# A two-layer graph network with a fast matrix product: one product at full width in the first pair, and new orders of the work

## The chip, the cores and the metric

The kernel runs on one core of one Trainium2 chip. TensorE (PE) multiplies matrices into PSUM, which has eight banks; VectorE (DVE) and ScalarE (ACT) read PSUM and work on SBUF; GpSimd (POOL) works on SBUF alone; SyncE (SP) issues all the DMAs. The metric is the device time of one execution in microseconds, lower being better.

## What is computed

There are 64 graphs, each with 256 nodes of 512 features (`x`), a dense 256x256 matrix `adj` and a mask. Two layers follow each other, all in fp32:

```python
# layer 0
agg = einsum('bij,bjf->bif', adj, x) / maximum(sum(adj, -1), EPS)
x   = layernorm(x + relu(concat([x, agg]) @ W.T))
# layer 1
q, k = split(x @ Wqk, 2);  v = x @ Wv
agg = einsum('bij,bjd->bid', adj, k * mask)
w   = inv_scale * mask * einsum('bid,bid->bi', q, agg)
x   = layernorm(x + softmax(w, axis=1)[:, :, None] * v)
```

The kernel uses that the aggregation commutes with the weights. Before the loop it multiplies the two halves of Wqk into one 512x512 matrix, so that in both layers a graph needs one product of its 512 features with a weight 1024 wide, one aggregation over the nodes, and vector work.

## The kernel before

**Pairs.** The graphs are worked two at a time: 32 pairs, the loop `for j in range(NP)`. In step j, layer 0 of pair j and layer 1 of pair j-1 run interleaved. Step 0 has layer 0 alone; after the loop comes layer 1 of the last pair alone.

**Fast products.** Each layer's weight product is split into 2x2 blocks and done with seven block products P1 to P7 in place of eight (`layer0`, `layer1`, `product`). Five of them, P1 to P5, are split once more in the same way (`inner`): seven matmuls of 256 columns in place of four of 512. P6 and P7 run at full width (`outer`, four matmuls of 512 columns). The price is sums: of the input blocks on POOL (`inner_sums`, `fourth_sums`, `outer_sums`), of the weights once at the start (`weight_sums`: `t1`, `t2`, `t4`, the in-place `b12`, and for each inner product the three arrays i1, i2, i4 and an in-place change of its upper right quarter), and of the results on DVE and ACT, which read one PSUM bank and add into another or into SBUF. The aggregation has seven products as well (`gather`).

**Letters.** The order of the matmuls is written out by hand as strings. Each letter takes the next piece of a product. In layer 0: i is P1, k P5, m P2, p P6, q P7, r P3, s P4, and a to g are the aggregation. In layer 1: J is P1, K P2, H P6, Q P7, N P5, P is product P4, L P3, and A to G the aggregation. S turns the last pair's scores into one row for its softmax, and Z turns the result back. I write K5 for the fifth of the seven pieces of K. The results of pieces 1, 3 and 5 of an inner product are put into the two accumulator banks by DVE or ACT; pieces 4, 6 and 7 (in this order behind 1, 3 and 5) then add their products to the same places by TensorE, so each waits for that add or copy.

**Order of the other engines.** `Plan` records every instruction. `Plan.order` then lists them with a model of costs: TensorE follows the strings nearly (an instruction may pass another by a little), and DVE, ACT, POOL and SP get an order from due times that are worked out backwards from TensorE's. This order is fixed in the program. `waiting` holds work that is recorded once certain letters are used up: `when("QP", ...)` runs after the last Q and the last P.

**Banks.** `HOME` and `HOME9` (last pair) give each letter the bank in which its pieces are made. Only the inner products and the aggregations read these entries. p, q, H and Q are `outer` products, which write straight to the banks of their results.

**Softmax and norms.** `softmax(j-2)` and `norm0(j)` are chains that pass between DVE (sums, `shift`), ACT (`less`, squares into `junk`, `rstd` by a logarithm and an exponential, scaling) and SP. `softmax_last` and the lines after `take(ORDER9, ...)` are the end of the kernel: scores from the last pieces of P, S, a maximum on DVE, exponentials on ACT, Z, then `stt` (add probability times v), a norm, and the stores. `sums_T` makes the combinations of a pair's rows that E and other aggregations read.

Of the kernel before, what the change touches and what calls it, by code (L numbers as in the profile page):

```python
# [16 lines left out]
P = 128  # L17
Q = 32
# [7 lines left out]
INNER = (("P1", "P2", "P5", "P3", "P4"), ("P1", "P2", "P5", "P3", "P4"))  # L26
SLOTS_X = {"P1": 0, "P2": 1, "P5": 2, "P3": 2, "P6": 0, "P7": 1, "P4": 0}
SLOTS_X1 = {"P1": 0, "P2": 1, "P5": 2, "P6": 0, "P7": 1, **({"P3": 2, "P4": 0} if "P7" in INNER[1] else {"P3": 0, "P4": 1})}
W1_BY_GP = ("P5", "P3", "P4")
HOME = "i6 k7 m6 p5 q1 r7 s6 a7 b2 c3 J6 K2 H3 Q5 N7 L7 P6 A6 B4 C5"  # L30
HOME9 = "J6 K6 H3 Q7 N7 L5 P1 A2 B3 C1"
LATE = 4.0
ORDER0 = ("i k i i k k i i i k i k k p m m m m k p m p p m q q r q s q r r s m s s r s s r r r a b s d e g "
          "c f")
ORDER1 = ("i k i k i i k i k i k k i k p m p q p r m q p m m r m s r q m r m q r s s r s r s J J J J s a J "
          "b J s d e c f J H g K K H K K K K N H N N K N H A Q Q D C N E N G P Q Q F P P N P P P B L P L L "
          "L L L L")
ORDER = ("i i k i i i k i i k k p m k m k k p p m r q p r q r q r m m r r s m m q s r s s s J a b s J J J "
         "J J s d e J c H f H K K K K g K Q N K N Q K A H D N C E H G N F Q Q N N B N L L L P P P P L P P "
         "L P L L")  # L40
ORDER9 = ("A J C D E J J G J J J J K B H H K K H N N H Q Q K N Q N F N N K K K Q P P P P P P P N L S L Z L "
          "L L L L")


class Step:
# [274 lines left out]
def resnorm_kernel(  # L320
# [13 lines left out]
    B, N, F = x.shape  # L334
    A = wqk_t.shape[0] // 2
    NT, NF, NA = N // P, F // P, A // P
    H, HF = NF // 2, F // 2
# [63 lines left out]
    def v_of(j):  # L401
        return shared[:, 2 * N_SIDE:].rearrange("p (k t f) -> p k t f", k=2, t=NT)
# [56 lines left out]
    for bank in (*banks[0], *(b for pair in banks for b in pair)):  # L459
        mm(bank.rearrange("p (a n) -> p a n", n=P), ones,  # L460
           ones[:, None, :].to_broadcast([P, F // P, P]), start=True)

    def weight_sums(w, name, layer, by_gp=()):
        b11, b21, b12, b22 = (w[:, k * H:(k + 1) * H, :] for k in range(4))
        t1, t2, t4 = (mem.tile([P, H, F], F32, name=f"{name}{k}") for k in (1, 2, 4))
        it = [mem.tile([P, len(INNER[layer]), HF], F32, name=f"{name}i{r}") for r in (1, 2, 4)]
        sides = {"P4": t4, "P6": t2, "P7": b12}
        sub = vec.tensor_sub

        def inner_of(p, b):  # L470
            if p not in INNER[layer]:
                return
            n = INNER[layer].index(p)
            sub = gp.tensor_sub if p in by_gp else vec.tensor_sub
            c11, c12, c21, c22 = (b[:, e, h * HF:(h + 1) * HF] for e in range(2) for h in range(2))
            i1, i2, i4 = (i[:, n] for i in it)
            sides[p] = {"B11": c11, "B21": c21, "B22": c22, "T3": c12, "T1": i1, "T2": i2, "T4": i4}
            sub(i1, c12, c11)
            sub(i2, c22, i1)
            sub(c12, c22, c12)  # L480
            sub(i4, c21, i2)
        sub(t1, b12, b11)
        inner_of("P1", b11)
        sub(t2, b22, t1)
        inner_of("P5", t1)
        sub(b12, b22, b12)
        sub(t4, b21, t2)
        inner_of("P2", b21)
        inner_of("P6", t2)
        inner_of("P7", b12)  # L490
        inner_of("P3", b22)
        inner_of("P4", t4)
        return sides
# [111 lines left out]
        return [first, common, second, second_row, third, fourth_sum, last]  # L605

    def product(layer, p, X, sides, w, q, done, onto=None):
        if p in INNER[layer]:
            return inner(p, X, sides, w, q, lambda: [done(k) for k in range(2)], onto)
        return outer(q, 0, X, BLOCK[p], sides[p], done) + outer(q, 1, X, BLOCK[p], sides[p], done)  # L610

    def outer(ps, k, X, slot, b, done=None):
        def unit(e):
            def go():
                mm(ps[k], X.chunk(slot, k, e), b[:, e])
                if e == H - 1 and done:
                    done(k)
            return go
        return [unit(e) for e in range(H)]
# [294 lines left out]
    W1 = weight_sums(w1, "t1_", 1, W1_BY_GP)  # L914
# [5 lines left out]
    for j in range(NP):  # L920
        X = Xs.pop(j)
        own = owns[j] = ring("own", [P, 2, NT, F], 3)
        u, y, o = pf, py, pu
        ys[j] = ring("y", [P, 2, NT, F])
        at = homes(HOME)
        units, made = layer0(j, X, o, u, y, at), Counter()
        sizes = Counter({name: len(parts) for name, parts in units.items()})
        waiting = []

        def when(done, work):  # L930
            waiting.append((full(done, sizes), work))

        def start_gather0():
            units.update(gather("abcdefg", sumsA.pop(j), sums_T(ys[j]), at["a"], at["c"], at["b"],
                                own=own, rdeg=rdegs.pop(j)))

        def end_gather0():
            place = norm0(j)
            mask_adj(j)
            if place:  # L940
                when("P.L" if j else "", place)

        def x_sums(*ps):
            for p in ps:
                if p in INNER[0]:
                    inner_sums(X, p)

        def next_x():
            if j == 0:
                pass  # L950
            elif j < NP - 1:
                load_xT(j + 1)
            if j < NP - 1:
                inner_sums(Xs[j + 1], None)
                outer_sums(Xs[j + 1], gp)
                inner_sums(Xs[j + 1], "P5")

        def next_adj():
            if j < NP - 1:
                load_adj(j + 1)  # L960
                sumsA[j + 1] = adj_sums(j + 1, 0)
        if j > 0:
            load_x(j)
        if 0 < j < NP - 1:
            load_rows(j + 1)
            degrees(j + 1)
        when("k", lambda: (fourth_sums(X), x_sums("P3")))
        when("i", lambda: x_sums("P6"))
        when("m", lambda: x_sums("P7"))
        when("p" if "P6" in INNER[0] else "i", lambda: x_sums("P4"))  # L970
        when("pqr", start_gather0)
        when("rs", next_x)
        when("abcdefg", end_gather0)
        if j == 0:
            when("abcdefg", next_adj)
        else:
            Y = x1Ts.pop(j - 1)
            u2, o2, y2 = o, pf, y
            vs[j - 1], aggs[j - 1] = v_of(j - 1), agg_of(j - 1)
            q_at = ys[j][:, :, 0]  # L980
            new, dots = layer1(j - 1, Y, q_at, o2, u2, y2, at)
            sizes.update({name: len(parts) for name, parts in new.items()})
            made["L"] = sizes["L"] - len(ahead)
            ahead += new.pop("L")
            units.update(new, L=ahead)

            def y_sums(*ps):
                for p in ps:
                    if p in INNER[1]:
                        inner_sums(Y, p)  # L990

            def start_layer1():
                if j == 1:
                    for k in range(2):
                        turn_here(Y, owns[0], k, o)
                    mask_adj(0)
                else:
                    softmax(j - 2)
                sumsM[j - 1] = adj_sums(j - 1, 1)
                inner_sums(Y, None)  # L1000
                outer_sums(Y, vec)
                inner_sums(Y, "P5")

            def start_gather1():
                units.update(gather("ABCDEFG", sumsM.pop(j - 1), T[0], at["A"], at["C"], at["B"],
                                    aggs[j - 1]))
            when("L" if j > 1 else "m", start_layer1)
            when("J", lambda: y_sums("P6"))
            when("K", lambda: y_sums("P7" if "P7" in INNER[1] else "P4"))
            when("H", lambda: (fourth_sums(Y), y_sums("P4" if "P7" in INNER[1] else "P3")))  # L1010
            if "P7" in INNER[1]:
                when("HN", lambda: y_sums("P3"))
            T = []
            when("ikmpqrs" if j == 1 else "", lambda: T.append(sums_T(owns[j - 1], aggs[j - 1])))
            when("gK", start_gather1)
            when("BFK", dots)
            when("ABCDEFG", next_adj)
        take((ORDER0, ORDER1)[j] if j < 2 else ORDER, units, made, waiting)
        if j > 0:
            py, pu = pu, py  # L1020

    j = NP - 1
# [11 lines left out]
    vs[j] = ring("x", [P, 2, NT, F])  # L1034
    at = homes(HOME9)
    units, dots = layer1(j, X, q_at, o, u, y, at)
# [18 lines left out]
    def divide():  # L1055
# [12 lines left out]
        ("BFK", dots))]  # L1068
    take(ORDER9, units, Counter(), waiting)
    p = small("probs", [P, 2, NT], 2)  # L1070
# [51 lines left out]
```

## Time and profile before

| | |
|---|---|
| median of 3 runs | 1848.31 us (1848.0 to 1849.67) |
| the profiled execution | 1848.66 us, with a span of 1846.6 us from first to last instruction |
| granted TensorE clock | 0.997 |
| instructions | 26243, of which 7382 are matmul records |
| ACT busy | 1245.6 us (67%) |
| POOL busy | 994.2 us (54%) |

An fp32 matmul leaves two records. From start to start, a record of 256 columns takes 0.216 us where nothing waits, and one of 512 columns takes 0.429 us; the TensorE timeline shows both throughout. So a matmul of 256 columns costs 0.43 us and one of 512 costs 0.86 us. The duration that the profile gives a record (0.38 us for 256 columns) [...] overlaps the next.

In the steady part, one step takes 56 us. The first 20 us are the product of Wqk's halves, while its data arrive. Step 0 is over at about 47 us and step 1 at about 113 us; the loop ends at about 1803 us, and the last pair takes the rest.

### The profile page before, as it was taken

To read this page: it belongs to the slowest core of one execution; us is meant where nothing else is said; L and a number is where in the kernel's file an instruction comes from. 1 tells how busy PE (TensorE), PEld (TensorE's weight loads), DVE (VectorE), ACT (ScalarE), POOL (GpSimd) and SP (SyncE) were. 2 spreads that over 40 slices of the span, in tenths; PEclk is the share of its full clock that TensorE was granted. 3 is DMA by queue.
4 is the path that set the end of the run, shared out by engine and by line. 5 is a ranking of instruction groups with operands and counts; after the bars stand their busy time and mean duration, and the time that the engine had idled before them with its cause. 6 is when DMAs were issued, how large, how long until landed. Compare 5 with 4: busy or idle time off the path is not lost.

```text
span 1846.6 us, 26243 instructions
## 1 busy us (share of the span) xinstructions
PE 1827.3 (99%) x7382; PEld 1383.0 (75%) x7382; DVE 1526.3 (83%) x3402; ACT 1245.6 (67%) x3243; POOL 994.2 (54%) x1523
## 2 busy tenths in 40 slices
PE   9999999999999999999999999999999999999997
PEld 5767777777777777777777777777777777777775
DVE  7887879788889888888888887887888888988876
ACT  3656776667766668766677766687666776666775
POOL 5755464564554664545655545655546545456432
PEclk9999999999999999999999999999999999999998
DMA  6134324343333343343433343433333433334311
GB/s 238 49 75 116 93 78 110 98 110 101 99 87 98 98 120 93 86 108 88 109 104 101 84 107 90 120 96 92 99 97 99 110 98 87 102 93 115 99 34 52
DMA packets 380720, 181.61 MB, mean 98 GB/s; under 512 B 263712, under 2 KB 345248, under 8 KB 380576
## 3 DMA queue, kind: packets, MB, share of 16 engines
q1 hardware_dynamic: 380576, 179.94, 36.2%
q8 instruction: 59, 0.97, 0.2%
q14 instruction: 85, 0.70, 0.1%
HBM read 114.35 MB, written 34.08 MB: 80 GB/s over the span
## 4 chain that ended last, share of the span: by engine, by line
PE 95%; DVE 3%; ACT 1%; DMA 1%; issue 0%; SPq 0%; DVEq 0%; ACTq 0%
PE bank L369 95%; DVE own L284 1%; DVE bank L284 1%; DMA shared<-wqk_t 1%; ACT junk L284 0%; DVE y L284 0%; ACT own L284 0%; PE bank L375 0%; DVE shared L284 0%; SPq L385 0%; DVE turn L284 0%; ACT shared L284 0%; DVE x L284 0%; ACT fifth L284 0%; ACT y L284 0%
## 5 line engine op out<-in xcount | busy, mean ns | idle before, releaser
L284 DVE TENSOR_TENSOR bank<-bank,fifth 128x256 f32<-128x256 f32 (+1 forms) x576 | 256.3, 455 | 137.2 <-ACT fifth L284 64.9
L284 ACT COPY y<-bank 128x512 f32<-128x512 f32 x256 | 149.4, 585 | 299.1 <-PE bank L369 268.2
L284 POOL TENSOR_TENSOR x1T_i<-x1T 128x128 f32<-128x128 f32 (+1 forms) x128 | 85.5, 677 | 391.7 <-PE bank L369 383.8
L284 ACT COPY bank<-bank 128x256 f32<-128x256 f32 (+1 forms) x352 | 149.7, 426 | 131.0 <-DVE bank L284 76.1
L284 ACT COPY shared<-bank 128x512 f32<-128x512 f32 x314 | 181.5, 583 | 52.3 <-PE bank L369 47.4
L369 PE MATMUL bank<-w,x1T 128*128 128x512 f32 (+1 forms) x512 | 206.5, 486 | 0.0
L284 ACT ACTIVATE own<-own,shift,rstd 128x512 f32<-128x512 f32 x254 | 193.5, 814 | 8.5 <-DVE shift L284 8.5
L369 PE MATMUL bank<-w,xT 128*128 128x256 f32 (+1 forms) x496 | 195.9, 486 | 0.2
L284 ACT ACTIVATE junk<-own,less 128x512 bf16<-128x512 f32 x254 | 183.4, 722 | 3.7
L284 DVE SCALAR_TENSOR_TENSOR own<-bank,rdeg,own 128x256 f32<-128x256 f32 x384 | 173.0, 476 | 9.1 <-PE bank L369 4.2
L369 PE MATMUL bank<-t_i,x1T_i 128*128 128x256 f32 x640 | 180.2, 380 | 0.2
L284 ACT COPY fifth<-bank 128x256 f32<-128x256 f32 x384 | 137.9, 375 | 53.6 <-PE bank L369 52.6
L284 DVE TENSOR_TENSOR y<-bank,y 128x512 f32<-128x512 f32 x192 | 132.3, 689 | 46.4 <-PE bank L369 38.5
L369 PE MATMUL bank<-t_i,xT_i 128*128 128x256 f32 x640 | 168.6, 380 | 0.3 <-DVE y L284 0.3
L284 POOL TENSOR_TENSOR xT_i<-xT 128x128 f32<-128x128 f32 (+1 forms) x126 | 84.6, 671 | 154.0 <-PE bank L369 143.0
L369 PE MATMUL bank<-t,x1T_s 128*128 128x512 f32 (+1 forms) x384 | 164.0, 521 | 0.1
L369 PE MATMUL bank<-t,xT_s 128*128 128x512 f32 (+1 forms) x384 | 159.8, 524 | 0.0
L369 PEld LDWEIGHTS bank<-t_i,xT_i 128*128 128x128 f32 x640 | 120.6, 189 | 46.6 <-POOL xT_i L284 12.2
L369 PEld LDWEIGHTS bank<-t_i,x1T_i 128*128 128x128 f32 x640 | 118.0, 190 | 39.4 <-issue 16.3
L284 DVE TENSOR_TENSOR shared<-bank,shared 128x512 f32<-128x512 f32 (+1 forms) x157 | 136.0, 891 | 10.8 <-PE bank L369 8.5
L284 ACT COPY own<-bank 128x512 f32<-128x512 f32 x192 | 110.2, 594 | 9.3 <-PE bank L369 7.1
L284 POOL TENSOR_TENSOR sa<-adj 128x256 f32<-128x256 f32 x128 | 102.8, 806 | 25.1 <-PE bank L369 15.2
(170 smaller groups left out, 4493.0 us busy)
## 6 DMA issues: line engine op xcount, KB each, us to landing
x<-x SPq DMA_DIRECT2D x64, 512.0 KB, 3.7
xT<-x_t SPq DMA_DIRECT2D x62, 512.0 KB, 3.8
out<-own SPq DMA_DIRECT2D x62, 512.0 KB, 3.0
x1T<-turn SPq DMA_DIRECT2D x480, 64.0 KB, 2.1
turn<-adj SPq DMA_DIRECT2D x64, 256.0 KB, 3.6
adj<-adj_t SPq DMA_DIRECT2D x64, 256.0 KB, 3.5
turn<-dram SPq DMA_DIRECT2D x31, 264.0 KB, 5.1
shared<-wqk_t SPq DMA_DIRECT2D x4, 512.0 KB, 8.4
```

What stands on the lines that cost most here:

```text
L284: self.plan.record(self.name, lambda: call(out, *args, **kwargs), outs, ins, busy, done, port)
L369: plan.record("PE", lambda: nc.tensor.matmul(ps, a, b, start=start, stop=True, skip_group_check=True), [ps], [a, b], busy, busy + 0.165, w ...
```

## The change

Five things are changed.

1. `FULL_FIRST`: at the first use of the layer 1 products, P4 has no inner weight sums yet. `sides["P4"]` is then the plain array `t4`, and `product` takes `outer`: four matmuls of 512 columns. `inner_sums` for P4 is left out in that step too. (P7 is in the tuple, but it is not an inner product, so nothing follows from that.)
2. The four subtractions on POOL that make P4's inner weight sums are recorded in step 1 after the last Q and P, in place of in the setup. From pair 2's layer 1 on (step 2), P4 is an inner product as before.
3. `ORDER0`, `ORDER1` and `ORDER9` are new: steps 0 and 1 and the last pair.
4. `ORDER` is new as well: it sets steps 2 to 31.
5. `HOME` changes p, q, H and Q only, which nothing reads. `HOME9` changes K from place 6 to 7 and L from 5 to 1 (and H and Q).

```diff
-HOME = "i6 k7 m6 p5 q1 r7 s6 a7 b2 c3 J6 K2 H3 Q5 N7 L7 P6 A6 B4 C5"
-HOME9 = "J6 K6 H3 Q7 N7 L5 P1 A2 B3 C1"
+HOME = "i6 k7 m6 p2 q0 r7 s6 a7 b2 c3 J6 K2 H4 Q7 N7 L7 P6 A6 B4 C5"
+HOME9 = "J6 K7 H2 Q1 N7 L1 P1 A2 B3 C1"
 LATE = 4.0
-ORDER0 = ("i k i i k k i i i k i k k p m m m m k p m p p m q q r q s q r r s m s s r s s r r r a b s d e g "
-          "c f")
-ORDER1 = ("i k i k i i k i k i k k i k p m p q p r m q p m m r m s r q m r m q r s s r s r s J J J J s a J "
-          "b J s d e c f J H g K K H K K K K N H N N K N H A Q Q D C N E N G P Q Q F P P N P P P B L P L L "
-          "L L L L")
-ORDER = ("i i k i i i k i i k k p m k m k k p p m r q p r q r q r m m r r s m m q s r s s s J a b s J J J "
-         "J J s d e J c H f H K K K K g K Q N K N Q K A H D N C E H G N F Q Q N N B N L L L P P P P L P P "
-         "L P L L")
-ORDER9 = ("A J C D E J J G J J J J K B H H K K H N N H Q Q K N Q N F N N K K K Q P P P P P P P N L S L Z L "
-          "L L L L")
+FULL_FIRST = ("P7", "P4")
+ORDER0 = ("k k k k k k i i i i i k i i p p q q r p p r r m m q m m r q m r m r s s s r s m a s b s d s e c "
+          "g f")
+ORDER1 = ("i k i i i i k k k i k k i p k m m p p r m q p m r m r q r s r q q s s m r s m s s a J s b d J "
+          "J e J J J J c H f H K H K g K Q K K K K C N A Q N N D H N N E N Q B Q P G P N L P L F L P L L L "
+          "L")
+ORDER = ("i i i k i i k k i i k k k k p p p r q p m m m r m q r m s q r q r s m s s r s s m r a J b J J d "
+         "J J J s e c J f H K K H K K g K K N Q K H N Q A D N C E N H Q N G N Q P P F P P P N L L L P P B "
+         "L L L L")
+ORDER9 = ("J J A D C E J J J J F J K G B H H K K K H Q K H N Q K Q K P Q N P N P N P P N P P S N N L L L L "
+          "Z L L L")
...
+    waiting_sums = {}
+
...
-        def inner_of(p, b):
+        def inner_of(p, b, later=None):
+            later = layer == 1 and p in FULL_FIRST if later is None else later
             if p not in INNER[layer]:
                 return
...
+            if later:
+                waiting_sums[p] = lambda: inner_of(p, b, False)
+                return
             sides[p] = {"B11": c11, "B21": c21, "B22": c22, "T3": c12, "T1": i1, "T2": i2, "T4": i4}
...
     def product(layer, p, X, sides, w, q, done, onto=None):
-        if p in INNER[layer]:
+        if p in INNER[layer] and isinstance(sides[p], dict):
...
-                    if p in INNER[1]:
+                    if p in INNER[1] and isinstance(W1[p], dict):
                         inner_sums(Y, p)
...
+            if j == 1:
+                when("QP", lambda: [waiting_sums[p]() for p in sorted(waiting_sums)])
```

**What the planner makes of it.** The built programs show the order of each engine's instructions (no times). TensorE's, at three places, before and then after (T is a transpose; a letter without number is an aggregation; in the last pair `:3` is the bank):

```
step 1, from J3 to E
before: J3 f T T T J5 f s6 J4 e J6 J7 e K1 s7 A K2 K4 K3 A g g K6 N1 N2 B
        H1 H3 H2 K5 H4 B K7 N3 D D N4 C C N5 N6 E E
after:  J3 c s7 c d d J4 J5 J6 e e f f J7 A A K1 K2 K4 H1 H3 H2 K3 H4 K5 K6
        K7 g g B Q1 N1 Q2 C N2 C Q3 N3 N4 Q4 N5 N6 B P1 D D P2 P3 E E

last pair, the end
before: P5:3 N6:0 P4:4 P6:4 N7:1 P7:5 L1:5 L2:5 S S S S L4:0 L3:5 L6:0 Z
        L5:5 Z Z Z L7:1
after:  P5:3 N1:7 K6:2 K4:2 N2:7 N3:7 P4:4 P6:4 P7:5 N5:7 N4:0 N6:0 S S S S
        N7:1 L1:3 L2:3 Z Z Z Z L4:0 L3:3 L6:0 L5:3 L7:1

steps 3 to 30, around N3 (after): ... K7 N2 Q2 G G N3 Q3 N5 P1 Q4 ...
DVE there (after): shift (of sum 2), shift (of sum 3), N3's add, turn, N5's add
```

In the last pair of the changed program, S uses banks 3 and 2, and L is made in bank 3. In steps 3 to 30 of the changed program every step of the same parity has the same order of TensorE; before, the planner's order varied from step to step. SP issues the same transfers; in the setup the two of `adj`'s rows come after the two of `adj_t` in place of around them.

More of the change, by code (lines that the diff above doesn't have):

```diff
@@ L29 @@
 W1_BY_GP = ("P5", "P3", "P4")
-HOME = "i6 k7 m6 p5 q1 r7 s6 a7 b2 c3 J6 K2 H3 Q5 N7 L7 P6 A6 B4 C5"
-HOME9 = "J6 K6 H3 Q7 N7 L5 P1 A2 B3 C1"
+HOME = "i6 k7 m6 p2 q0 r7 s6 a7 b2 c3 J6 K2 H4 Q7 N7 L7 P6 A6 B4 C5"
+HOME9 = "J6 K7 H2 Q1 N7 L1 P1 A2 B3 C1"
 LATE = 4.0
-ORDER0 = ("i k i i k k i i i k i k k p m m m m k p m p p m q q r q s q r r s m s s r s s r r r a b s d e g "
-          "c f")
-ORDER1 = ("i k i k i i k i k i k k i k p m p q p r m q p m m r m s r q m r m q r s s r s r s J J J J s a J "
-          "b J s d e c f J H g K K H K K K K N H N N K N H A Q Q D C N E N G P Q Q F P P N P P P B L P L L "
-          "L L L L")
-ORDER = ("i i k i i i k i i k k p m k m k k p p m r q p r q r q r m m r r s m m q s r s s s J a b s J J J "
-         "J J s d e J c H f H K K K K g K Q N K N Q K A H D N C E H G N F Q Q N N B N L L L P P P P L P P "
-         "L P L L")
-ORDER9 = ("A J C D E J J G J J J J K B H H K K H N N H Q Q K N Q N F N N K K K Q P P P P P P P N L S L Z L "
-          "L L L L")
+FULL_FIRST = ("P7", "P4")
+ORDER0 = ("k k k k k k i i i i i k i i p p q q r p p r r m m q m m r q m r m r s s s r s m a s b s d s e c "
+          "g f")
+ORDER1 = ("i k i i i i k k k i k k i p k m m p p r m q p r m r m r q r s r q q s s m r s m s s a J s b d J "
+          "J e J J J J c H f H K H K g K Q K K K K C N A Q N N D H N N E N Q B Q P G P N L P L F L P L L L "
[5 more added lines that the diff above has]
+          "Z L L L")
 class Step:
```

## The prediction

> **What bounds the kernel now.** I read the page first, then windows, TensorE's waits, the timelines of the places that stood out, and the chain of waits.
>
> ```profile
> PE 1827.3 (99%) x7382; PEld 1383.0 (75%) x7382; DVE 1526.3 (83%) x3402; ACT 1245.6 (67%) x3243; POOL 994.2 (54%) x1523
> ...
> PE 95%; DVE 3%; ACT 1%; DMA 1%; issue 0%; SPq 0%; DVEq 0%; ACTq 0%
> ```
>
> TensorE is busy nearly all the time, and the chain that ended last is 95% TensorE. So only two things count: how long the matmuls are, and where TensorE stands still. The matmuls alone: 6272 records of 256 columns at 0.216 us, 1056 of 512 at 0.429, and small ones (9 us) make 1817 us. The span is 1846.6. Of the other 30 us, 1.1 lie before the first matmul and 7.6 after the start of the last; 21 are gaps. Windows show where:
>
> ```profile
> core 0: us, PE busy (x) PEld busy (x) DVE busy (x) ACT busy (x) POOL busy (x), PEclk, DMA share, GB/s
> ...
> 81.00:97.00 16.00, 15.60 (x61) 10.63 (x60) 12.52 (x22) 6.27 (x13) 13.36 (x21) 1.00 0.00 0
> 97.00:103.00 6.00, 3.93 (x17) 2.76 (x16) 5.00 (x10) 4.02 (x11) 5.92 (x7) 1.00 0.29 91
> 103.00:116.00 13.00, 12.39 (x49) 8.78 (x48) 11.62 (x25) 8.94 (x21) 5.12 (x9) 1.00 0.35 92
> ...
> 170.00:1827.00 1657.00, 1656.19 (x6725) 1264.24 (x6725) 1376.68 (x3090) 1137.48 (x2963) 890.40 (x1369) 1.00 0.36 96
> 1827.00:1847.00 20.00, 7.65 (x32) 4.40 (x30) 12.91 (x36) 10.16 (x31) 0.00 (x0) 0.75 0.28 105
> ```
>
> Steps 3 to 31 lose 0.8 us in this view, but a record's 0.38 us covers short gaps. I therefore took 0.216 or 0.429 from each distance between starts and summed by step: setup 1.6 us, step 0 0.6, step 1 6.1, step 2 1.3, steps 3 to 31 5.0 together (0.17 a step), last pair 6.5. The largest:
>
> ```profile
> 99.86 1.13 PE L369 MATMUL bank<-shared,sa 128*128 128x256 f32 x4 [2.07 <-ACT shared L284]
> ```
>
> That is E in step 1: D's copy stood on ACT behind a norm's squares, while DVE was still making the sums. The end, first TensorE, then DVE:
>
> ```profile
> 1827.61 0.59 PE L369 MATMUL bank<-t_i,x1T 128*128 128x256 f32 x2
> 1829.68 0.70 PE L369 MATMUL bank<-w,x1T_s 128*128 128x256 f32 x2 [1.47 <-DVE bank L284]
> ...
> 1838.40 1.22 PE L369 MATMUL bank<-t_i,x1T_s 128*128 128x256 f32 x2 [2.86 <-DVE bank L284]
> ```
>
> ```profile
> 1828.84 0.73 DVE L284 SCALAR_TENSOR_TENSOR bank<-bank,shared 128x512 f32<-128x512 f32 x1
> ...
> 1829.48 1.22 DVE L284 TENSOR_TENSOR x<-bank,x 128x1024 f32<-128x1024 f32 x1
> 1830.62 0.15 DVE L284 SCALAR_TENSOR_TENSOR w<-scores,mask_sb 128x4 f32<-128x4 f32 x1
> ...
> 1837.66 0.69 DVE L284 TENSOR_TENSOR bank<-bank,x 128x512 f32<-128x512 f32 x1
> ```
>
> L1 (1829.68) shares a bank with P7, which DVE reads until 1829.57. The scores' scaling (1830.62) stands behind a 1.22 us add, so S starts at 1830.92. L7 (1838.40) waits for L5's add.
>
> **What the Trainium skill says.** "PSUM — Partial Sum Buffer", "Engine vs sequencer instructions": ScalarE, VectorE and GpSimd queues are strictly first in, first out, and matmuls run in program order. The trace agrees: the 0.15 us scaling waited for the 1.22 us add. The same page, "PSUM bank collisions raise a hardware error": guard by bank, not by address; L1's 1.47 us is such a wait. "TensorE: Matmul & The Clock Gate", "What's actually happening": after an idle window of about 3.4 us the clock is halved. L7 took 1.22 us in place of 0.59, in a window with clock 0.75.
>
> **The change part by part.**
>
> *P4 at full width in step 1.* Removed: 7 x 0.43 = 3.0 us of matmuls; added: 4 x 0.86 = 3.4. Cost +0.4 us on TensorE. Gone with it: four ACT copies (0.375 each), five DVE adds (4 x 0.43 + 0.69 = 2.4 us) and four POOL sums (about 2 us), all off the path unless DVE is late there; I give nothing for them. The four weight subtractions move: 4 x 0.73 = 2.9 us of POOL leave the setup and return near step 1's P. Their first reader is the next step's P, some 56 us later, and POOL is 54% busy: nothing. If POOL were late, sums queued behind them would wait, 3 us at most, once.
>
> *HOME.* Only unread entries change: nothing. *SP* issues the same transfers; two of 256 KB swap places in the first 20 us, and their readers come after 19 us: nothing, at worst 0.5.
>
> *Steps 0 and 1.* Up to r3 step 0's order is the same, so its 0.5 us wait stays. In step 1 three things change. (a) Before E there are now 31 matmuls from K2 on, 11 of them of 512 columns: 20 x 0.43 + 11 x 0.86 = 18.1 us. DVE's work from K1's add to the last sum E needs is 21 operations, 12.6 us by medians and up to 15 with the slow ones of this stretch (own<-own,x took 1.22). So E no longer waits for sums: -2.3 us. ACT is nearer: from Q4's copy to D's I count 0.5+0.2+0.1+0.84+0.72+0.75+0.57 = 3.7 us plus about 0.5 for a `shift`, against 4.7 of matmuls: hidden, at worst 1 lost. (b) K is packed tighter. K1 needs the bank that f leaves, and DVE's list from J3's add to K1's holds 7.6 us, where TensorE has 6.9; K4 stands one matmul behind K1 and waits for its add (0.43 + 0.2 + queue); K7 stands one behind K5's add (0.69). I count 0.55 + 0.75 + 0.5, and 0.1 more for each restart: 2.3 us, against 1.4 lost between 83 and 90 us before: +0.9 (0 to +2). (c) Around i5 and k3 (1.4 us lost before) DVE's queue behind e's results is 9 x 0.41 + 0.43 us against 10 x 0.43 of matmuls: 0.3 to 0.6 lost, -0.9. At the passage to step 2 (1.4 us before: L5, i1, i4) the distances are one to three matmuls longer: 0.5 lost, -0.9. Sum: -2.3 + 0.9 - 0.9 - 0.9 = -3.2; I take -3.0, since a new order has short waits I can't see.
>
> *Steps 2 to 31.* For each matmul that waits for another engine I took the matmuls between it and its source, less the chain's durations from the trace. Before, 11 or 12 places a step have under 0.5 us left; after, five (k1, s3, J1, E, N5, 0.19 to 0.46). N5, with one 512 matmul behind N3, has the least, 0.19; in steps 10, 18 and 25 before it had the same and did not wait. So most of the 5.0 us goes: -2.0 (-4 to 0 by these distances alone; what a queue can do to N5 is below).
>
> *Last pair.* Four of N's matmuls that stood before P7 now stand behind it: 4 x 0.43 = 1.7 us earlier for P7 and all that follows. They fill the time in which DVE multiplies scores. By the DVE order: P6's and P7's dots (0.69, 0.73) now run at once, N5's add 0.43, scaling 0.15, and S starts 1.6 us after P7 issued (2.9 before). Then a 1.22 add, two maxima, exponentials; L1, now in S's bank, waits for the first exponential, about 1.0; Z ends some 5.4 us after P7 (7.4 before). But L4 to L7 now come after Z: L3's add (0.43), three `stt` (0.74 each) and L5's add lie in DVE's queue, and L5's add ends about 9.1 us after P7, against 10.3. Behind it all is as before. So -1.7 - 1.2 = -2.9 (-4 to -1).
>
> Sum: +0.4 - 3.0 - 2.0 - 2.9 = -7.5 us on a span of 1846.6. The profiled execution was 1848.66, so 1841.2; the median lies 0.35 lower: **1840.8 us**.
>
> **The rivals.** *Slower: a repeated wait at N5.* In steps 3 to 31 DVE must do the `shift` of the second norm sum just before N3's add, and `shift` needs ACT's last `rstd`.
>
> ```profile
> DVE shift L284 <- ACT rstd L284: 25.5, 20, 5.0
> ```
>
> So DVE has stood still there, up to 5.0 us. In step 13 before, with nearly this ACT order, the second exponential began at
>
> ```profile
> 777.20 0.21 ACT L284 ACTIVATE rstd<-rstd 128x2 f32<-128x2 f32 x1
> ```
>
> after N3's result (777.11), and cost nothing, as N3's add stood ahead of it. After the change K7's and G's copies differ: from the third square on I count 10.9 us of ACT without a pause, from 4.1 to 4.4 us after e starts, so it ends at 15.0 to 15.3, and N3's result is there at 15.7. The margin is 0.4 us, and the order is the same in 28 steps. If ACT is later than this by more than 0.4 us, each microsecond beyond costs 28 us: 0.4 beyond adds 11 (and the gain of these steps is lost): 1854. It turns the whole into a loss from about 0.25 beyond. For it: DVE's and ACT's order can't yield. Against it: a margin counted with measured durations, and a method that gives 16.7 for step 13, where 16.8 was measured.
>
> *No change to speak of.* The short waits come back elsewhere: K in step 1 loses 2 us more, E still waits 1 us for ACT, steady steps keep their 5 us, the end gains 2: 0.4 - 0.5 + 0 - 2 = about 1846. For it: DVE is 9.7 of 10 us busy around 78 to 88. Against it: the end's gain is plain order.
>
> *More.* Steady gaps vanish (-4), step 1 does a little better than summed (-3.7), end -3.5: +0.4 - 3.7 - 4 - 3.5 = -10.8, so 1837.5.
>
> **How the numbers follow.** A measurement of this kernel can tell about 0.2%, 3.7 us, from no change. Forecast (1838.5 to 1844) 0.60; more 0.12; little change (1844 to 1848) 0.16; slower by N5 or the like 0.12. Faster by over 0.2% (below 1844.6): 0.60 + 0.12 + a little of the third = 0.75; same 0.14; slower 0.11. Range 1836.5 to 1847.5: it leaves out the N5 case and the far end of the other.
>
> **What would show it.** Right: no gap over 1 us at E in step 1; S within 2 us of P7, L1 waiting about 1 us for ACT; gaps in steps 3 to 31 under 3 us in sum; a few tenths at K1, K4 and K7. Wrong: a gap before N5 in each step, led by DVE behind ACT's `rstd`; a gap at E of 2 us as before; an end no shorter than the 19.0 us that it took from P7's start before.

## The result, and the profile after

The changed kernel takes 1843.46 us (median of 8 runs, 1842.39 to 1845.7), the kernel before, beside it, 1848.99 us (1848.0 to 1850.43). The ratio is 0.9971, with a 95% interval of 0.9960 to 0.9981: 5.5 us less. The profiled execution has a span of 1842.4 us, 4.2 less than the one before. Part of the spread is TensorE's clock: of the 59 runs of the kernel before that stand beside the first experiments, 36 with a mean clock of 0.997 or 0.998 took 1847.6 to 1849.3 us and 23 with 0.996 took 1849.6 to 1851.7, and the changed kernel's eight runs split in the same way (below), so a median mixes two kinds of execution and a profile shows one of them.

The first and the fourth part of the page after, engines and the chain that ended last:

```profile
PE 1829.1 (99%) x7376; PEld 1381.8 (75%) x7376; DVE 1542.9 (84%) x3397; ACT 1243.4 (67%) x3239; POOL 957.5 (52%) x1519
...
PE 98%; DVE 1%; DMA 1%; ACT 0%; SPq 0%; issue 0%; DVEq 0%; ACTq 0%
```

The chain has gone from 95% to 98% TensorE, so fewer waits are left on the path. Windows of the kernel after, by stage (the first is the work on K in step 1, the last begins with P7's start):

```profile
core 0: us, PE busy (x) PEld busy (x) DVE busy (x) ACT busy (x) POOL busy (x), PEclk, DMA share, GB/s
...
82.00:93.00 11.00, 8.81 (x29) 4.98 (x29) 8.72 (x16) 3.31 (x7) 8.78 (x12) 1.00 0.00 0
93.00:108.84 15.84, 15.84 (x58) 10.51 (x57) 13.38 (x29) 11.77 (x29) 5.60 (x8) 1.00 0.22 69
...
164.00:1795.40 1631.40, 1631.39 (x6617) 1243.33 (x6616) 1376.11 (x3043) 1117.28 (x2918) 845.73 (x1354) 1.00 0.37 97
...
1822.70:1842.40 19.70, 10.20 (x37) 5.92 (x35) 13.70 (x39) 10.80 (x32) 0.00 (x0) 0.68 0.29 107
```

In this view TensorE has no pause from 93 us to the end of step 1, where E had waited 2 us. It pauses between 82 and 93 us instead, and in the last stage its mean clock is 0.68. In the long stage a record's duration hides short gaps, so I summed them as in the prediction, from start to start. A record made at half the clock counts its extra time as a gap:

| gaps of TensorE, us | before | after | change | forecast |
|---|---|---|---|---|
| setup | 1.56 | 1.56 | 0 | 0 |
| step 0 | 0.59 | 0.06 | -0.5 | 0 |
| step 1 | 6.12 | 4.03 | -2.1 | with step 2's start: -3.0 |
| step 2 | 1.25 | 0.11 | -1.1 | |
| steps 3 to 31 | 4.96 | 5.00 | 0 | -2.0 |
| last pair | 6.47 | 5.62 | -0.9 | -2.9 |
| matmuls themselves | 1816.8 | 1817.2 | +0.4 | +0.4 |
| sum | | | -4.2 | -7.5 |

The 0 in the row of steps 3 to 31 is this execution's. Four of the experiments below keep TensorE's order of steps 4 to 30 (the last pair undone, P4 split, small matmuls, L earlier), and their profiles show gaps of 5.5 to 5.9 us there; the old steady order, profiled three times (before, steps 0 and 1 alone, P4 alone), lost 4.8 to 5.0. So in these profiles the new steady order loses up to 1 us more than the old, not less.

TensorE's timeline after, where K is worked in step 1:

```profile
82.69 0.70 PE L370 MATMUL bank<-w,x1T 128*128 128x256 f32 x2 [0.65 <-DVE own L285]
...
84.41 0.70 PE L370 MATMUL bank<-w,x1T 128*128 128x256 f32 x2 [0.59 <-DVE bank L285]
85.67 2.81 PE L370 MATMUL bank<-t,x1T_s 128*128 128x512 f32 x6 [0.56 <-DVE x1T_s L285]
...
91.00 0.70 PE L370 MATMUL bank<-t_i,x1T 128*128 128x256 f32 x2 [0.36 <-DVE bank L285]
```

K1, K4, H1 and K7 each wait for DVE; with the restart behind each wait (the second record comes 0.075 or 0.104 us late) they lose 3.2 us of the 3.6 lost between K1 and E. And at the end, from P7 on:

```profile
1822.70 0.59 PE L370 MATMUL bank<-t_i,x1T 128*128 128x256 f32 x2
...
1825.05 0.60 PE L827 MATMUL bank<-ident,w 128*1 128x128 f32 x4 [0.21 <-DVE w L285]
...
1827.09 0.70 PE L370 MATMUL bank<-w,x1T_s 128*128 128x256 f32 x2 [1.01 <-ACT fifth L285]
...
1829.70 1.13 PE L370 MATMUL bank<-t_i,x1T_i 128*128 128x256 f32 x2
1831.35 2.08 PE L370 MATMUL bank<-w,x1T_i 128*128 128x256 f32 x4 [0.53 <-DVE bank L285]
1834.22 1.22 PE L370 MATMUL bank<-t_i,x1T_s 128*128 128x256 f32 x2 [0.79 <-DVE bank L285]
```

P7 starts 4.9 us earlier than before, S follows 2.35 us behind it (3.3 before; counted from P7's end, as in the prediction, 1.9 and 2.9), and L1 waits about 1 us for an exponential, as forecast. But L3 (1829.70), L6 with L5 (1831.35) and L7 (1834.22) run at half the clock: L7 takes 1.22 us in place of 0.70. From P7's start to the end it is 19.7 us, where the kernel before took 19.0.

### The profile page after: what moved, and what is told of

The parts are those of the page before. It is cut to its first block, busy times and chain, and to the rows that moved or that the text cites. A ratio compares the mean times of both kernels' runs of the same rounds, so it can differ in the third digit from the quotient of the medians.

```text
span 1842.4 us, 26290 instructions
## 1 busy us (share of the span) xinstructions
PE 1829.1 (99%) x7376; PEld 1381.8 (75%) x7376; DVE 1542.9 (84%) x3397; ACT 1243.4 (67%) x3239; POOL 957.5 (52%) x1519
## 4 chain that ended last, share of the span: by engine, by line
PE 98%; DVE 1%; DMA 1%; ACT 0%; SPq 0%; issue 0%; DVEq 0%; ACTq 0%
PE bank L370 97%; DMA shared<-wqk_t 1%; DVE bank L285 0%; DVE own L285 0%; PE bank L376 0%; SPq L386 0%; ACT own L285 0%; DVE w L285 0%; DVE y L285 0%; DVE x1T_s L285 0%; DVE t L285 0%; ACT fifth L285 0%; DVE x L285 0%; ACT junk L285 0%; ACT bank L285 0%
## 5 line engine op out<-in xcount | busy, mean ns | idle before, releaser
L285 DVE TENSOR_TENSOR bank<-bank,fifth 128x256 f32<-128x256 f32 x571 | 255.7, 454 | 50.3 <-ACT fifth L285 22.9
L285 POOL TENSOR_TENSOR x1T_i<-x1T 128x256 f32<-128x256 f32 (+1 forms) x126 | 74.8, 605 | 409.4 <-PE bank L370 399.9
L370 PE MATMUL bank<-w,xT 128*128 128x256 f32 (+1 forms) x496 | 200.1, 486 | 0.0
L285 ACT ACTIVATE own<-own,shift,rstd 128x512 f32<-128x512 f32 x254 | 197.9, 820 | 1.5 <-DVE shift L285 1.5
L370 PE MATMUL bank<-t,xT_s 128*128 128x512 f32 (+1 forms) x384 | 153.8, 521 | 0.0
L285 POOL TENSOR_TENSOR sa<-adj 128x256 f32<-128x256 f32 x128 | 93.7, 732 | 99.0 <-ACT adj L285 94.5
L285 DVE TENSOR_TENSOR shift<-less,rstd 128x2 f32<-128x2 f32 (+1 forms) x128 | 46.4, 380 | 113.6 <-ACT rstd L285 113.5
L285 POOL TENSOR_TENSOR xT_i<-xT 128x128 f32<-128x128 f32 (+1 forms) x126 | 80.2, 637 | 114.3 <-PE bank L370 103.3
L370 PEld LDWEIGHTS bank<-t_i,x1T_i 128*128 128x128 f32 x636 | 120.1, 190 | 19.7 <-issue 2.2
```

The lines of the kernel that those rows point to most:

```text
L285: self.plan.record(self.name, lambda: call(out, *args, **kwargs), outs, ins, busy, done, port)
L370: plan.record("PE", lambda: nc.tensor.matmul(ps, a, b, start=start, stop=True, skip_group_check=True), [ps], [a, b], busy, busy + 0.165, w ...
```

## The experiments

Two theories stood at the start. A: the gain lies in steps 0 to 2; the new steady order only trades many different short waits for two that repeat; at the end half of what P7 wins is lost again. The rival: the sizes of the forecast, with 4.9 of 7.9 us from the steady order and the last pair. From P4 split on, A and the rival are what each expectation calls so. The runs of each group below shared the runs of the kernel before on their chip.

**Steps 0 and 1 alone.** `ORDER`, `ORDER9` and `HOME9` are those of before:

```diff
-HOME9 = "J6 K7 H2 Q1 N7 L1 P1 A2 B3 C1"
+HOME9 = "J6 K6 H3 Q7 N7 L5 P1 A2 B3 C1"
...
-ORDER = ("i i i k i i k k i i k k k k p p p r q p m m m r m q r m s q r q r s m s s r s s m r a J b J J d "
...
+ORDER = ("i i k i i i k i i k k p m k m k k p p m r q p r q r q r m m r r s m m q s r s s s J a b s J J J "
...
```

> The changed kernel with the old ORDER, ORDER9 and HOME9: only steps 0 and 1 are new, with P4 at full width. Theory A (the gain of 5.5 us lies in steps 0 to 2): 2.5 to 3.5 us below before, no gap at E, gaps in step 1 near 4.0 us against 6.1, steps 3 to 31 near 5.0 us as before, end as before. Theory B (it lies in the steady order and the last pair, as 4.9 of the 7.9 us that were forecast did): 0.5 us or less below before.

Measured: 1844.37 us against 1848.78, ratio 0.9974 (0.9963 to 0.9985), 4.4 us less; gaps of steps 0 to 2 4.0 us (8.0 before), steps 3 to 31 4.8, last pair 6.47. So most of the gain needs neither the new steady order nor the new end. Theory A holds here, the size a little above it.

**The steady order alone.** Only `ORDER` is taken over into the kernel before.

> The kernel before with the new ORDER alone. Theory A (the many different waits of the old steps were replaced by small waits that repeat in each step, at k2 and N5): gaps of steps 3 to 31 stay at 5.0 us within 0.5, the time within 1 us of before. The forecast's theory (few tight places, few gaps): 2 us less in these steps, 1846 to 1847 us.

Measured: 1851.04, ratio 1.0010 (1.0003 to 1.0016), 2.3 us more. Gaps of steps 3 to 31 are 6.2 us (5.0 before), the last pair 7.4 (6.5): behind the new last step the old `ORDER9` waits 0.45 us at P7 and 0.2 longer at L1. The forecast's -2.0 for these steps falls.

**The last pair undone.** The changed kernel with the old `ORDER9` and `HOME9`; TensorE's order up to step 30 is untouched.

> The changed kernel with the old ORDER9 and HOME9: the last pair alone is undone. Theory A (of the 1.7 us by which P7 comes earlier about half is lost again behind Z): 0.7 to 1.2 us above the changed kernel, so about 4.5 us below before. The forecast's sizes: 2.9 us above the changed kernel, 2.5 us below before.

Measured: 1847.63, ratio 0.9993 (0.9987 to 1.0000). Against the changed kernel's ratio of 0.9971 that is some 4 us, nearer to the forecast than to theory A. Gaps of the last pair are 8.6 us against 5.6. Of these 2.9 us about one comes from the clock, which in this execution was halved for 3.4 us around S (S's records 0.216 us apart in place of 0.108). So the new last pair is worth more than theory A gave it, since the old one fits the new steady order badly.

**P4 alone.** The kernel before with P4 at full width and its weight sums later; all other orders old, with three P's taken out:

```diff
...
-          "b J s d e c f J H g K K H K K K K N H N N K N H A Q Q D C N E N G P Q Q F P P N P P P B L P L L "
...
+... N G P Q Q F P N P B L P L L L L L L
```

> The kernel before with P4 at full width in step 1 (three P's less in the old ORDER1) and its weight sums later; all other orders old. Theory A (width costs its matmuls, what it frees on DVE, ACT and POOL is not on the path): 0.4 us more for matmuls, gap at E still 1.5 us or more, time 0 to 1 us above before. Rival (the relief of DVE and ACT is itself what takes E's wait away): gap at E below 0.7 us and the time 1 to 2 us below before.

Measured: 1847.05, ratio 0.9987 (0.9981 to 0.9994), 1.7 us less, the rival's size. But not by its mechanism: gaps of step 1 rose from 6.1 to 7.5 us. TensorE's timeline of this run, at K:

```profile
85.21 0.71 PE L368 MATMUL bank<-t_i,x1T_i 128*128 128x256 f32 x2 [1.72 <-DVE y L283]
86.78 2.04 PE L368 MATMUL bank<-t,x1T_s 128*128 128x512 f32 x2 [0.87 <-DVE x1T_s L283]
...
89.47 1.91 PE L368 MATMUL bank<-tv,adj 128*128 128x256 f32 x4
```

E no longer waits, since the planner put three pieces of Q, N7 and two of L ahead of it. DVE's backlog is paid at K, and behind those waits the clock is halved (g, 89.47, takes 1.91 us where 1.03 is usual; the mean between 82 and 93 us is 0.69). That costs time of its own: the five runs with a mean clock of 0.997 or 0.998 took 1844.9 to 1845.9 us, the sixteen with 0.996 took 1846.6 to 1848.7. The waits at the passage to step 2 (1.4 us before, at L5, i1 and i4) are gone. P4's four matmuls stand behind K, and three of them behind E. So its width probably acts on K and E through the planner, which works due times out backwards; this was not tried apart.

**P4 split under the new orders.** The reverse: `FULL_FIRST` is empty, three P's are added to `ORDER1`. TensorE's order from step 3 to the end is that of the changed kernel.

```diff
-FULL_FIRST = ("P7", "P4")
+FULL_FIRST = ()
...
-... N E N Q B Q P G P N L P L F L P L L L L
+... N E N Q B Q P P G P N P L P P L F L P L L L L
```

> The changed kernel with P4 split in step 1 too (its weight sums back in the setup, three P's more in the new ORDER1); from step 3 to the end TensorE's order is that of the changed kernel. Theory A (width costs 0.4 us of matmuls, but the work on DVE, ACT and POOL that goes with it was in the way of step 0, of K and of the passage to step 2): gaps of steps 0 to 2 5.5 to 7 us against 4.2, the time 1 to 2.5 us above the changed kernel. Rival (the gain of steps 0 to 2 is all due to the new orders): gaps within 0.5 us of the changed kernel's, time 0.4 us below it.

Measured: 1840.8 us (1839.96 to 1842.81), ratio 0.9955 (0.9942 to 0.9967). Theory A falls: the gaps of steps 0 to 2 are 3.1 us, below the changed kernel's 4.2, and the matmuls 0.4 less. Together that is 1.5 us. Around K 1.2 us are lost in place of 3.5, and E still waits for nothing. So under the new orders the full width is a loss, and most of what is lost around K in the changed kernel comes with it. In this profile P7 starts only 0.5 us earlier, as setup and steady steps happened to lose 0.9 more; the other 1.8 of the 2.3 between the two profiles come from the last pair, where this execution kept its clock (below). The median, 2.7 us below the changed kernel's, therefore holds both.

**The last pair with small matmuls in its waits.** The finished list of instructions is edited; nothing else moves. `fill` multiplies the identity into a bank that nothing reads afterwards, 128 columns, 0.22 us each:

```diff
+        for n, piece in ((4, ("N", 7)), (3, ("L", 3)), (4, ("L", 5))):
+            for _ in range(n):
+                s = Step("PE", self.fill, 0, 0, False, 0, ())
...
+                self.move([s], behind=self.found("PE", *piece, 32))
```

> The changed kernel with eleven small matmuls (128 columns of the identity into an unused bank, 0.22 us each) put where TensorE waits in the last pair: four before L1, three before L6, four before L7. Theory A (the halved clock lies on the path: L3, L6 with L5 and L7 took 1.13, 2.08 and 1.22 us in place of 0.59, 1.02 and 0.70): the clock stays at 1.0 until L7, the end is 18.0 to 18.8 us after P7's start in place of 19.7, 1.0 to 1.7 us below the changed kernel. Rival (DVE sets the pace there, the clock is only seen beside it): clock 1.0 and less than 0.4 us gained.

Measured: 1842.87 (1842.62 to 1842.97), ratio 0.9964 (0.9952 to 0.9977). Its TensorE timeline, L3, L6 with L5, and L7:

```profile
1830.14 0.64 PE L394 MATMUL bank<-t_i,x1T_i 128*128 128x256 f32 x2
...
1831.30 1.13 PE L394 MATMUL bank<-w,x1T_i 128*128 128x256 f32 x4
...
1833.45 0.70 PE L394 MATMUL bank<-t_i,x1T_s 128*128 128x256 f32 x2
```

The clock stayed at 1.0 until the last matmul, and the end is 17.9 us behind P7's start (1841.1 - 1823.2), against 19.7. In the profiles that is theory A, 1.8 us. The median gains only 0.6 (1.3 by the ratios, whose intervals overlap), because the changed kernel does not lose its clock in each run. P4 split has the changed kernel's order of TensorE here, without small matmuls, and in its profile the clock falls only behind L7 (0.70 us). Its window from P7's start to the end:

```profile
1822.16:1840.10 17.94, 8.21 (x37) 5.01 (x35) 13.60 (x39) 10.73 (x32) 0.00 (x0) 0.89 0.32 118
```

17.9 us again, and so in the two runs with exchanges on DVE below, while the run with exchanges on TensorE lost its clock and took 19.9. The changed kernel's own eight runs agree: the five with a mean clock of 0.998 or 0.999 took 1842.4 to 1843.9, the three with 0.996 or 0.997 took 1844.1 to 1845.7.

**L earlier in the last pair.** L is made in P7's second bank; L4 and L3 go ahead of Z on TensorE, L5 ahead of L6, and DVE's adds for L1, L3 and L5 move forward with them.

> The changed kernel with L of the last pair made in P7's second bank, in place of the one that S uses, so that L1 needs no exponential; L4 and L3 stand ahead of Z on TensorE, L5 ahead of L6, and DVE does L1's, L3's and L5's adds that much earlier. All else is in the same order. Theory A (the end is held by L's chain behind S and Z): L1 starts within 0.5 us of N7, L7 at most 9.5 us after P7's start (11.5 in the changed kernel), the end 17.5 to 18.5 us after P7's start (19.7), 1.2 to 2.2 us below the changed kernel. Rival (DVE's own work behind Z sets the end): L7 earlier, but the end less than 0.6 us earlier.

Measured: 1843.56, ratio 0.9969 (0.9957 to 0.9980), the changed kernel's time within the interval. L7 starts 9.5 us behind P7, as theory A had it, and the end comes 18.5 behind it. But L2 waited for L1's add, which I had put between the two in one bank, and the clock fell again (L7 1.22 us). The end is still later than the 17.9 us that the untouched order takes with its clock kept. DVE is busy 14.1 of the 15 us from 1821 on, which suggests that with the chain shortened it is DVE that holds the end. Neither theory is settled in full.

**Both ends new, the steady order old.** The changed kernel with the `ORDER` of before.

> The changed kernel with the old ORDER: steps 0 and 1 and the last pair new, the steady steps old. Theory A (the new ORDER brings nothing by itself): gaps of steps 4 to 30 4.3 to 5.0 us, last pair 5.0 to 6.0, time within 0.8 us of the changed kernel, near 1843.5. Rival (the new last pair pays only behind the new ORDER, whose last step hands it its sums earlier): last pair 6.5 us or more, 1844.5 to 1846.

Measured: 1920.2 us, ratio 1.0385 (1.0371 to 1.0399). Neither theory had this. The planner, starting from a different end, makes a steady order in which gaps of steps 3 to 31 are 76 us; the total of TensorE's waits:

```profile
PE bank L370 <- DVE bank L285: 39.3, 27, 1.9
```

In 21 steps L4 follows L1 too closely and waits up to 1.9 us for L1's add. With the old end and with the new steps 0 and 1, the same string gave 4.8 us. So the new `ORDER` does bring something that no sum over its own gaps shows: in all runs with it the planner made the same steps 4 to 30, whatever stood at the ends.

**Two neighbours exchanged on TensorE.** In steps 3 to 31 P1 goes ahead of N5, and k2 ahead of i5; the other engines keep their order.

> The changed kernel with two neighbours exchanged on TensorE in each of steps 3 to 31: P1 ahead of N5, and k2 ahead of i5. All other engines keep their order. Theory A (4.2 of the 4.7 us of gaps in steps 3 to 30 are these two places, each short by 0.1 us or less, plus the restart behind it): gaps of steps 3 to 31 fall from 5.0 to 1.5 us or less, 3 to 4 us below the changed kernel. Rival (DVE sets the pace, so the wait moves on to the next reader): they fall by less than 1.5 us.

Measured: 1862.39, ratio 1.0071 (1.0058 to 1.0083). Each step now loses 0.84 us in place of 0.17: k2 waits 0.18, i7 (behind the later i5) 0.21, P1 0.05, and each restart costs 0.1. The rival holds, and more: N5's neighbour is as tight as N5.

**Two exchanges on DVE.** Why N5 waits is seen in step 13 of the changed kernel, DVE and then POOL:

```profile
772.05 0.18 DVE L285 TENSOR_TENSOR shift<-less,rstd 128x2 f32<-128x2 f32 x1 [3.55 <-ACT rstd L285]
772.63 0.70 DVE L285 TENSOR_TENSOR shift<-less,rstd 128x2 f32<-128x2 f32 x1 [0.40 <-ACT rstd L285]
773.25 0.42 DVE L285 TENSOR_TENSOR bank<-bank,fifth 128x256 f32<-128x256 f32 x1
```

```profile
772.59 0.73 POOL L285 TENSOR_TENSOR xT_i<-xT 128x256 f32<-128x256 f32 x1
```

The second `shift`, 2 columns wide, takes 0.70 us and ends with POOL's sum. Step 12 is the other case, again DVE and then POOL:

```profile
716.50 0.16 DVE L285 TENSOR_TENSOR shift<-less,rstd 128x2 f32<-128x2 f32 x1 [0.29 <-ACT rstd L285]
```

```profile
716.55 0.75 POOL L285 TENSOR_TENSOR xT_i<-xT 128x256 f32<-128x256 f32 x1
```

Over steps 3 to 30 the trace splits cleanly: in 10 steps this `shift` took 0.16 to 0.18 us, as it had begun 0.05 us or more ahead of POOL's sum, and N5 did not wait; in the other 18 it took 0.67 to 0.77, N3's add began 0.12 to 0.20 us later behind N3 than in the ten, and N5 waited 0.03 to 0.11 us with 0.075 for the restart. N5 itself began 0.66 us behind that add in the ten steps and 0.57 behind it in the eighteen, so it has 0.09 us to spare. This execution was a lucky one: in the four others with this order the `shift` was slow in 25 to 27 of the 28 steps. So N3's add was put ahead of this `shift`, and the add for i3 ahead of the product of scores:

```diff
+        for j in range(3, 31):
+            for letter, name in (("N", "shift"), ("i", "bank")):
...
+                self.move([add], ahead=[ahead])
```

> The changed kernel with two exchanges on DVE in each of steps 3 to 30, TensorE's order untouched: N3's add goes ahead of the shift before it (which took 0.70 us in step 13 in place of 0.12), and the add for i3 ahead of the product of scores before it. Theory A (N5 and i5 are late by what stands ahead of these adds on DVE): gaps of steps 3 to 30 fall from 4.7 to 2 us or less, 2 to 4 us below the changed kernel. Rival (as with the exchange on TensorE, what was put behind is then late itself: ACT's scaling behind the shift, or P's bank behind the product): gaps stay at 4.5 us or grow.

Measured: 1854.22, ratio 1.0027 (1.0016 to 1.0037). N5's wait was gone in all 28 steps. But i4 waited 0.44 us in each: it writes the bank that the add for i3 now used ahead of it. So the second exchange was made the other way, the product behind the add:

```diff
-                self.move([add], ahead=[ahead])
+                if letter == "N":
+                    self.move([add], ahead=[ahead])
+                else:
+                    self.move([ahead], behind=[add])
```

> As the run before, but the product of scores goes behind the add for i3 in place of the add ahead of it, so that i4's matmul stays ahead of that add (i4 writes the same bank; with the add ahead of it, it had waited 0.44 us in each step). Theory A (N5 and i5 are late by what stands ahead of these adds on DVE): i4 does not wait, gaps of steps 3 to 30 fall from 4.7 to between 0.7 and 2 us, 2.5 to 4 us below the changed kernel, 1839.5 to 1841. Rival (what was put behind, the product or ACT's scaling, is late in turn): gaps above 4 us, no gain.

Measured: 1858.01, ratio 1.0051 (1.0038 to 1.0063). N5's wait is gone again, DVE there now reading:

```profile
778.54 0.23 DVE L315 TENSOR_TENSOR shift<-less,rstd 128x2 f32<-128x2 f32 x1 [3.50 <-ACT rstd L315]
779.60 0.43 DVE L315 TENSOR_TENSOR bank<-bank,fifth 128x256 f32<-128x256 f32 x1 [0.83 <-PE bank L400]
779.94 0.35 DVE L315 TENSOR_TENSOR shift<-less,rstd 128x2 f32<-128x2 f32 x1
```

But the add for i3 stood still 0.65 us until i4 had left its bank, the product behind it came late, then ACT's copy for k1, and k2 waited 0.5 us in each step. So theory A is right for N5 and wrong for i5, whose 0.06 us did not go either. The exchange at N5 without the other was not run.

**All together.** P4 split, both DVE exchanges in their second form, and the small matmuls.

> P4 split in step 1 too, the two exchanges on DVE of the run beside it, and the eleven small matmuls that keep the clock up in the last pair. If the three gains add (1.5 us in steps 0 to 2 with the matmuls, 2.5 to 4 in the steady steps, 0.6 to 1.8 at the end): 1836.5 to 1838.5 us. If the steady exchange fails: 1840 us.

Measured: 1856.03 (1855.86 to 1856.23), ratio 1.0038 (1.0024 to 1.0052). The steady exchange spoils it as in the run beside it. Against that run, on the same chip, it is 2.0 us faster, with no overlap of the runs. The last stage from P7's start to the end, first that run's, then this one's (columns as in the windows above):

```profile
1837.98:1855.90 17.92, 8.20 (x37) 5.01 (x35) 13.59 (x39) 10.74 (x32) 0.00 (x0) 0.83 0.32 118
1836.37:1854.30 17.93, 10.51 (x59) 7.93 (x57) 13.59 (x39) 10.73 (x32) 0.00 (x0) 0.94 0.32 118
```

The stage is equally long in both, since the clock fell behind the last matmul in both, and P7 starts 1.6 us earlier. So in the profiles the small matmuls brought nothing here and the gain is that of P4 split; they can only help in a run that would lose its clock.

## Why the prediction was right, and where not

*P4's matmuls*, +0.4: measured +0.41. "I give nothing" for the rest of this part: under the old orders it came with 1.7 us less, under the new ones with some 1.5 more, it seems through the order that the planner then makes. What the weight sums alone do where they are put was not tried.

*Steps 0 and 1*, -3.0: measured -3.8, right in sign, in a different split.
- E's wait went, as counted from 18.1 us of matmuls against DVE's 12.6 to 15 (-2.3).
- "K is packed tighter", +0.9 (0 to +2): measured about +2, the far end. K1, K4 and K7 wait as named: 0.82, 0.76 and 0.52 us, with 0.55, 0.75 and 0.5 counted. (With three restarts at 0.1 the sum is 2.1 us, not 2.3.) H1's 0.80 was not seen: its sum on DVE took 1.26 us where 0.68 is usual. So from K1 to E 3.6 us are lost against 3.9, and the backlog has moved rather than gone.
- i5 and k3, -0.9: measured -1.1.
- The passage to step 2, -0.9: measured -1.2, and 0.5 more at the passage to step 3.
- "Its 0.5 us wait stays" in step 0 was wrong: -0.5. The wait is gone with P4 alone too, where `ORDER0` is the old one, and back (0.46 us) in the run with both ends new and the steady order old. So it belongs to the planner's whole list, not to the string of step 0.

*Steps 2 to 31*, -2.0: measured 0 in steps 3 to 31, and up to +1 in other executions. This step failed, in two places. N5 lost 2.5 us: it was rightly named the tightest, but had 0.09 us to spare and not 0.19, and durations "from the trace" stood for operations whose duration has two values. A `shift` at 0.16 to 0.18 leaves N5 its margin; one at 0.70 doesn't. The rival "a repeated wait at N5" had named the place and the instruction, but ACT's `rstd` is half of the reason: in step 13 it released the `shift` at 772.60, and the half microsecond more came from POOL's sum, begun at 772.59. N5 was late by at most 0.11 us, so it cost 2.5 us with the restarts and not 11. The other place, i5, was not among the five tight ones that were listed: it lost 0.06 us in each of 28 steps, 1.7 us, and why stays open, since the exchange on DVE did not take it away.

*The last pair*, -2.9: measured -0.9 in the profile. The first term, 1.7 us for N's matmuls behind P7, is right: P7 came 4.9 us earlier, of which steps 0 to 2 with P4 gave 3.4. The second, -1.2, was 19.0 to 17.8 us from P7's start; with the clock kept it is 17.9. In this execution it was 19.7, as L3 to L7 ran at half the clock. I had noted the halved clock at L7 in the profile before and left it out of the sum after. An end no shorter than 19.0 us had been named as a sign of being wrong, and in this execution it was seen. So the mechanism was right, and a term of up to 1.8 us was missing, which comes in some runs only: by their mean clock, in three of eight.

Together: -7.5 forecast, -4.2 in the profile, -5.5 in the medians; the two missing sizes are the steady 2.0 and the clock, and steps 0 to 2 gave 0.8 more. In part that was luck: the 0.5 us of step 0 were not foreseen, and the parts could be summed only because the planner kept the steady steps with this end. With the same new end and the old `ORDER` it did not, and the time was 1920 us.

## What to carry to other kernels

Before a margin of tenths is trusted, look at the spread of each operation in front of it, not at its median: one operation of 2 columns had two durations here, 0.17 and 0.70 us, and which came was decided by 0.05 us. Where TensorE waits about a microsecond at a time, price the matmuls that follow at both clocks. And where a planner turns strings into queues, an edit is worth what the whole list that it leads to is worth: the same string gave 4.8 or 76 us of gaps in the steady steps.

## What the runs showed of the hardware that was not expected

- The clock of TensorE was halved without a long pause: in the changed kernel at about 1829.6 us, after waits of 0.4 and 1.2 us, while the same order kept it in three other kernels' runs. The Trainium skill, "TensorE: Matmul & The Clock Gate", "What's actually happening", says that the window in which activity is watched is about 3.4 us long and free-running, not tied to the kernel's start. The traces agree: the clock was halved for 3.41 us with the old last pair (from 1828.58 on) and for 6.83, twice as long, with P4 alone (from 85.77), and in the changed kernel it had been full for 1822.72 us, 534 times 3.413. Counted from P7's start, the changed kernel's windows began about 0.25 us earlier than those of the run with P4 split, which kept its clock. How much work in a window keeps the clock no run here settles.
- A DVE operation on 2 columns took 0.70 us while POOL worked on a sum. The skill's "SBUF — State Buffer", "Who interferes with whom", describes a port pair that one of the two holds for the whole instruction, with a DVE operation on two SBUF inputs among those that contend. The 18 slow and 10 quick cases agree: it was quick where it began 0.05 us or more ahead of POOL's sum. That the port is the cause was not tested by moving POOL's sum.
- The first matmul behind even a short wait loses 0.075 to 0.10 us more at its second record, so the 18 short waits at N5 cost as much in restarts (1.35 us) as in waiting (1.19 us).
